# A graph kernel on one Trainium2 core: row sums and norm applications at fixed places of ScalarE's order, one eviction moved to ScalarE, one VectorE operation in four

## The chip, the cores and the metric

The kernel runs on one core of one Trainium2 chip. The core has five engines that work side by side: TensorE (PE in the profile; its weight loads are PEld), VectorE (DVE), ScalarE (ACT), GpSimd (POOL) and SyncE (SP), which here only issues DMA transfers. SBUF is the working memory, PSUM the memory that TensorE writes. The metric is the device time of one execution in microseconds (us), as the median of the runs.

## The reference

There are 64 graphs of 256 nodes with 256 features, x and adj being 64 x 256 x 256 in float32. Two layers run, each with a residual and a layer norm:

```python
# layer 0
deg = adj.sum(axis=-1); deg = jnp.where(deg != 0, deg, 1.0)
d = deg ** -0.5
a_plus = d[:, :, None] * adj * d[:, None, :] + max(alpha, MIN_VALUE) * eye
x = layernorm(x + einsum('bnf,pf->bnp', einsum('bnm,bmf->bnf', a_plus, x), W) + b)
# layer 1
h = relu(bn1(x @ conv1))                     # 1-tap convolution over features
x_conv = relu(bn2(conv17(h over nodes)) + x) # 17 taps, padding 8
s = x @ w_se.T + b_se                        # 3 columns
A = exp(-(|s_n|^2 + |s_m|^2 - 2 s_n . s_m))
msg = relu(x @ w_msg.T + b_msg)
x_in = concatenate([x_conv, A @ msg])
r, z = sigmoid(gi_r + gh_r), sigmoid(gi_z + gh_z)  # gi = x_in @ w_ih.T + b_ih, gh = x @ w_hh.T + b_hh
x = layernorm(x + (1 - z) * tanh(gi_n + r * gh_n) + z * x)
```

## The kernel before, in words

A tile has 128 partitions, so a graph's 256 nodes and its 256 features are two chunks each. The graphs go in four batches of Q = 16, because the 17-tap convolution is done through frequencies for 16 graphs at once.

`layer0(g)` is a generator, and each `yield` ends a piece. Its first piece sums adj's rows (`degrees()`, L357: two ScalarE operations of 256 columns, each followed by a read of its accumulator), corrects deg on VectorE (L368), raises it to -1/2 on GpSimd (dis, L370), takes alpha times deg (L372), transposes adj (TensorE L379, evicted by ScalarE L380), adds the diagonal (VectorE L382), scales x by dis on ScalarE (L392, twice) and adds a bias to the loaded x on GpSimd (L393). Then come p_hT (L400, evicted by L405), p_out (L410, evicted on VectorE by L415), and the layer norm. `layernorm` takes statistics on VectorE (L326 to L328), a power on GpSimd (ln_rs, L329), then ln_mr on VectorE (L332) and the application on ScalarE (L334, twice). Last, ScalarE's queue issues the store of x1 (L421).

`x1_transposed(g)` transposes the normed graph (L430) into one PSUM tile and evicts it by two operations into xn: xn's first part on VectorE (L434), or on ScalarE (L432) if the graph is in ALONE, and its last part on ScalarE (L435). `layer1(g)` multiplies by the conv weights (p_conv, L450, evicted per chunk by ScalarE as h, L453, and scols, L454), squares scols for the distances on VectorE (L458 to L461), makes messages (p_msg L471, ReLU L474), transforms to frequencies (p_dft L486, evicted by L491), transposes scols (p_rows L499, evicted as dist_l L501 and dist_r L503), takes distances (p_dist L510), their exponential (L511) and product with adj (L512), and p_nmp (L519, evicted by L523, stored by L524).

After a batch, `products` multiplies frequencies by the convolution's weights u, which are loaded from DRAM (p_k, L545; VectorE and ScalarE evict by L587 to L590, butterflies L595 and L596), `real_transform` (from L651 on, its last line L677 one VectorE operation of 8 x 256 = 2048 columns) and `complex_begin` and `complex_end` transform back, and the convolution's output goes to DRAM (xc_d). `gru(g)` then computes the gates of a graph by eight products p_g (L871) of three matmuls of 384 columns each, some on sums of blocks that GpSimd makes (L842). Its evictions are first (ScalarE L882), L888, L889, L898, L900 on VectorE, and quarter(0,0) (ScalarE L891). Tanh is on ScalarE (L913, L929), the rest on VectorE (L921 to L938). The graph's last norm is left in NORMS, and `ended()` applies it (L332, L334) and issues the store of out (L849) within the next graph's gru.

`graphs` drives a batch: for each graph it walks layer1's seven pieces, and after some of them runs a piece of layer0 of the graph two ahead (PLACES) or of other work, such as gates. After the piece APPLIED (the products for p_rows) it runs ENDS, which is layer 0's pending norm with its store. Graphs 16 to 27 (ALONE) are begun alone beside the first batch's products; graphs 32 to 37 and 48 to 53 are begun ahead beside later products, with their frequencies in a second tile V2 that L1104 copies. `paced` puts pieces of the inverse transforms behind marked operations. Within an engine a scheduler decides the order when the program is built, from the order in the program and a model of durations; the engines' queues are then fixed. `tc.issue_after(ins)` binds what is issued under it to come after ins in the order of ins's own engine. PSUM evictions share two pools of four banks; `bank` takes them in turn.

Time runs in stages: set-up with graphs 0 to 15 (to 280 us), the first products beside graphs 16 to 27 (to 460), graphs 28 to 31 with first gates (to 600), second products (to 720), gates beside graphs 32 to 37 (to 930), gates beside 38 to 47 (to 1120), the same for the third batch (to 1630), the last products (to 1720) and the last gates.

Of the kernel before, what the change touches and what calls it, by code (L numbers as in the profile page):

```python
# [10 lines left out]
AF = mybir.ActivationFunctionType  # L11
ALU = mybir.AluOpType
AX = mybir.AxisListType

P = 128
# [11 lines left out]
def kernel(  # L27
# [27 lines left out]
    nc = tc.nc  # L55
    B, N, D = x.shape
    TAPS = conv2T.shape[1]
    PAD = TAPS // 2
    NSE = w_seT.shape[1]
# [8 lines left out]
    Q = P // GT  # L68
# [22 lines left out]
    def mark(op, gates=0):  # L91
        marks.append((op.ins, gates))
# [248 lines left out]
    xn_d = [dram.tile([P, 2 * DCH, N], F32, name=f"xn_d{g}") for g in range(B)]  # L341
    XN = {}
    ALONE = set()
    ADJT, X1, X_SCALED, DIAGONAL = {}, {}, {}, {}


    def layer0(g):

        a_t, x_t = ain.pop(g), xin.pop(g)

        adjT = work.tile([P, NCH, 3, P], F32, name="adjT", bufs=3)
        ADJT[g] = adjT

        deg = small.tile([P, NCH], F32, name="deg")
        def degrees():
            for c in range(NCH):
                nc.scalar.activation(  # L357
                    unused if g >= Q else adjT[:, c, 0:2, :].rearrange("p n q -> p (n q)"), a_t[:, c, :], AF.Copy,
                    accum_out=deg[:, c : c + 1],
                )  # L360

        if g == 1:

            with tc.issue_after(X_SCALED[0]):
                degrees()
        else:
            degrees()
        nc.vector.scalar_tensor_tensor(deg, deg, 0.0, deg, op0=ALU.is_equal, op1=ALU.add)  # L368
        dis = small.tile([P, NCH], F32, name="dis")
        nc.gpsimd.tensor_tensor(dis, deg, neg_half[:, :NCH], op=ALU.pow)  # L370
        adeg = small.tile([P, NCH], F32, name="adeg")
        nc.vector.tensor_scalar(adeg, deg, alpha_t, None, op0=ALU.mult)  # L372

        p = bank("p_adjT").rearrange("p (c n) -> p c n", c=NCH)
        for mc in range(NCH):
            for c in range(NCH):
                nc.tensor.transpose(p[:, mc, c * P : (c + 1) * P], a_t[:, c, mc * P : (mc + 1) * P], ident)  # L379
        copied = nc.scalar.copy(adjT[:, :, 0:3:2, :], p.rearrange("p c (n q) -> p c n q", q=P))  # L380
        for mc in range(NCH):
            DIAGONAL[g] = nc.vector.scalar_tensor_tensor(  # L382
                adjT[:, mc, 1, :], ident, adeg[:, mc : mc + 1], adjT[:, mc, 2 * mc, :],
                op0=ALU.mult, op1=ALU.add,
            ).ins


        x1 = work.tile([P, NCH, D], F32, name="x1")
        X1[g] = x1
        with tc.issue_after(copied.ins) if g < 2 else ExitStack():  # L390
            for c in range(NCH):
                X_SCALED[g] = nc.scalar.activation(x1[:, c, :], x_t[:, c, :], AF.Copy, scale=dis[:, c : c + 1]).ins  # L392
        nc.gpsimd.tensor_tensor(x_t, x_t, b0_t.unsqueeze(1).to_broadcast([P, NCH, D]), op=ALU.add)  # L393

        yield
        hT = work.tile([P, DCH, N], F32, name="hT", bufs=1)
        p = bank("p_hT").rearrange("p (k n) -> p k n", k=DCH)
        for k in range(DCH):
            for mc in range(NCH):
                nc.tensor.matmul(  # L400
                    p[:, k, :], x1[:, mc, k * P : (k + 1) * P],
                    adjT[:, mc, 1 - mc : 3 - mc, :].rearrange("p n q -> p (n q)"),
                    start=mc == 0, stop=mc == NCH - 1,
                )
        nc.scalar.copy(hT, p)  # L405
        yield
        p = bank("p_out0").rearrange("p (c o) -> p c o", c=NCH)
        for c in range(NCH):
            for k in range(DCH):
                nc.tensor.matmul(  # L410
                    p[:, c, :], hT[:, k, c * P : (c + 1) * P], w0[:, k, :], start=k == 0, stop=k == DCH - 1
                )
        for c in range(NCH):
            mark(
                nc.vector.scalar_tensor_tensor(  # L415
                    x1[:, c, :], p[:, c, :], dis[:, c : c + 1], x_t[:, c, :], op0=ALU.mult, op1=ALU.add
                )
            )
        yield
        yield from layernorm(x1)  # L420
        nc.scalar.dma_start(x1_d[g // Q][g % Q].rearrange("(c p) d -> p c d", p=P), x1)  # L421
        yield

    def x1_transposed(g, alone=False):
        x1 = X1.pop(g)
        xn = XN[g] = work.tile([P, 2 * DCH, N], F32, name="xn")
        p = bank("p_x1T").rearrange("p (k n) -> p k n", k=DCH)
        for k in range(DCH):
            for c in range(NCH):
                nc.tensor.transpose(p[:, k, c * P : (c + 1) * P], x1[:, c, k * P : (k + 1) * P], ident)  # L430
        if alone:
            nc.scalar.activation(xn[:, 0], p[:, 0], AF.Identity, bias=unit, scale=others_only)  # L432
        else:
            nc.vector.tensor_scalar(xn[:, 0], p[:, 0], others_only, unit, op0=ALU.mult, op1=ALU.add)  # L434
        nc.scalar.copy(xn[:, 2 * DCH - 1], p[:, 1])  # L435

    def layer1(g, place):
# [3 lines left out]
        xn, adjT = XN.pop(g), ADJT.pop(g)  # L441
# [5 lines left out]
        for c in range(NCH):  # L447
            p = bank("p_conv1")[:, : D + NSE]
            for k in range(DCH):
                nc.tensor.matmul(  # L450
                    p, x1T[:, k, c * P : (c + 1) * P], wc1[:, k, :], start=k == 0, stop=k == DCH - 1
                )
            nc.scalar.activation(h[:, c, :], p[:, :D], AF.Relu)  # L453
            nc.scalar.copy(cols[:, c, :, :NSE], p[:, D:].unsqueeze(1).to_broadcast([P, 4, NSE]))  # L454

        s3 = cols[:, :, 0, :NSE]
        sq3 = small.tile([P, NCH, NSE], F32, name="sq3")
# [11 lines left out]
        for c in range(NCH):  # L469
            for k in range(DCH):  # L470
                nc.tensor.matmul(  # L471
                    p[:, c, :], x1T[:, k, c * P : (c + 1) * P], wmsg[:, k, :], start=k == 0, stop=k == DCH - 1
                )
        mark(nc.scalar.activation(msg, p, AF.Relu))  # L474
        yield


# [34 lines left out]
        mark(nc.vector.tensor_mul(aT, aT, adjT[:, :, 0:3:2, :]))  # L512
        yield
        if g in ALONE:
            x1_transposed(g + 1, True)
        p = bank("p_nmp").rearrange("p (k n) -> p k n", k=DCH)
        for k in range(DCH):
            for mc in range(NCH):
# [132 lines left out]
    def real_transform():  # L651


        sub2(M[:, 0:3:2, :], M[:, 1:4:2, :])
        yield

        sub2(M[:, 4:6, :].rearrange("p a o -> p (a o)"), M[:, 6:8, :].rearrange("p a o -> p (a o)"))
        add2(M[:, 6, :], M[:, 7, :])
        r = math.sqrt(0.5)
        for i, by in enumerate((-1.0, 1.0, -r, r)):  # L660
            stt(M[:, 4 + i, :], M[:, 4 + i, :], by, M[:, i, :], op0=ALU.mult, op1=ALU.add)
        stt(M[:, 0:4, :], M[:, 0:4, :], 2.0, M[:, 4:8, :], op0=ALU.mult, op1=ALU.subtract)
        yield

        run(four(8, 12))
        yield
        nc.vector.tensor_sub(M[:, 8, :], M[:, 0, :], M[:, 8, :])
        nc.vector.tensor_add(M[:, 12, :], M[:, 4, :], M[:, 12, :])
        for i, x, y in ((1, 9, 13), (2, 10, 14), (3, 15, 11)):
            angle = math.pi * ORDER[i] / 8  # L670
            t = freq.tile([P, 2, D], F32, name="turn", bufs=2)
            by = real_part(t[:, 0, :], M[:, x, :], M[:, y, :], angle)
            imaginary_part(t[:, 1, :], M[:, x, :], M[:, y, :], angle)
            stt(M[:, 8 + i, :], t[:, 0, :], -by, M[:, i, :], op0=ALU.mult, op1=ALU.add)
            stt(M[:, 12 + i, :], t[:, 1, :], by, M[:, 4 + i, :], op0=ALU.mult, op1=ALU.add)
            yield
        stt(M[:, 0:8, :], M[:, 0:8, :], 2.0, M[:, 8:16, :], op0=ALU.mult, op1=ALU.subtract)  # L677
        yield

    CR, CI = 16, 32  # L680
# [170 lines left out]
    def ended():  # L851
        while NORMS:
            run(NORMS.pop(0))

    def gru(g):
# [21 lines left out]
        def quarter(c, h):  # L877
            return G[:, c, h].rearrange("p t d -> p (t d)")
# [9 lines left out]
        mark(nc.vector.tensor_add(quarter(0, 1), first, p6), 1)  # L888
        nc.vector.tensor_add(quarter(1, 1), quarter(0, 1), p7)  # L889
        product(A12, B21, p1)  # L890
        nc.scalar.copy(quarter(0, 0), p1)  # L891
        yield
        if following:
            transposed(g + 1)
        ended()
        load_x1(g)
        p5 = product(S[1], T1)
        mark(nc.vector.tensor_add(quarter(1, 1), quarter(1, 1), p5), 1)  # L898
# [69 lines left out]
    def run(stage):  # L968
        for _ in stage:
            pass  # L970
# [21 lines left out]
    def graphs(first, part, others):  # L992


        for i in part:
            load(first + i + 3)
            given = {"layer0": layer0(first + i + 2) if first + i + 2 < B else iter(()), "other": others[i]}
            for piece, _ in enumerate(layer1(first + i, i)):
                if piece == APPLIED:
                    run(ENDS.pop())  # L1000
                    ENDS.append(given["layer0"])
                elif piece == STATS:
                    next(given["layer0"], "end")
                yield
                for name in PLACES[piece]:
                    if next(given[name], "end") != "end":
                        yield
            yield from given["other"]
# [203 lines left out]
```

## Time and profile before

| | |
|---|---|
| three runs | 2105.25, 2107.64, 2108.99 us, median 2107.64 |
| profiled execution | 2108.64 us |
| its span | 2106.8 us, so 1.8 around it |
| granted TensorE clock | 0.989 |
| matmuls | 8157 |
| L357 on the unused tile | 96 of 0.415 us, and 96 reads of 0.189 |
| L334 on x, on x_g | 128 of 0.601, 128 of 0.596 us |
| L434 (VectorE), L432 (ScalarE) | 52 of 0.533, 12 of 0.564 us |
| L677, L596 with 512 columns | 4 of 2.286, 68 of 0.755 us |
| L370 (dis), L392 | 64 of 0.719, 128 of 0.509 us |

Times are those of one profiled execution, in us from the start of its span. A busy share is the time in which an engine ran instructions. In the view of waits a line names the engine that stood still and its instruction, then who released it, and the total, the number and the longest of such waits. A timeline has a line for each instruction or run of alike ones: start, duration, engine, line of the kernel, what it writes and reads, how many, and in brackets the idle time ahead of it with its releaser. TensorE's ends are modelled, so that a matmul that waits inside a run shows as a longer run.

### The profile page before, as it was taken

The page shows a single profiled execution, that of the slowest core. Times are in us where ns is not written, and L with a number is a line of the kernel's source. Part 1 is how long each engine was busy: PE and PEld are TensorE (multiplying, and loading weights), DVE is VectorE, ACT ScalarE, POOL GpSimd, SP SyncE. Part 2 cuts the span into 40 slices and gives each one's busy share as a digit, 9 for nine tenths or more (in the row PEclk, how much of TensorE's full clock was granted, in tenths as well). Part 3 has the DMA queues.
Part 4 walks back from the last instruction along what each step waited for, and adds up shares of the span by engine and source line. Part 5 has one row for each costly group of instructions (what it writes and reads, how often), then busy time and mean ns, then how long its engine had stood idle before and what let it go on. Part 6 is the DMA issues. An engine that isn't in the chain of part 4 may idle for free. (4 is left out here: it accounts for less than half of the span.)

```text
span 2106.8 us, 26312 instructions
## 1 busy us (share of the span) xinstructions
PE 2004.8 (95%) x8157; PEld 1444.7 (69%) x8157; DVE 1437.3 (68%) x3281; ACT 923.4 (44%) x2180; POOL 668.0 (32%) x672
## 2 busy tenths in 40 slices
PE   6999999999999999999999999999999999999997
PEld 5888778877677766767677666667767765555554
DVE  5545467776567788863446888875444899976776
ACT  4666643566431234455453123546544123333333
POOL 3444410122332243322322234323222124434442
PEclk9999999999999999999999999999999999999999
DMA  4765557545346644343326655434322845443331
GB/s 125 226 217 183 190 173 228 176 140 155 92 149 201 203 126 120 115 118 108 101 86 189 195 155 140 120 110 120 109 83 90 254 142 147 115 117 97 93 94 54
DMA packets 305289, 298.05 MB, mean 141 GB/s; under 512 B 84192, under 2 KB 283956, under 8 KB 305150
## 3 DMA queue, kind: packets, MB, share of 16 engines
q1 hardware_dynamic: 245198, 200.37, 32.7%
q10 hardware_dynamic: 44480, 67.39, 9.0%
q0 software_dynamic: 15472, 28.61, 6.2%
q8 instruction: 66, 1.08, 0.2%
q14 instruction: 73, 0.60, 0.1%
HBM read 193.19 MB, written 103.06 MB: 141 GB/s over the span
## 5 line engine op out<-in xcount | busy, mean ns | idle before, releaser
L871 PE MATMUL p_g<-wall,sums 128*128 128x384 f32 x1536 | 541.4, 493 | 8.0 <-DVE G L898 8.0
L871 PEld LDWEIGHTS p_g<-wall,sums 128*128 128x128 f32 x1536 | 286.3, 192 | 199.4 <-issue 17.6
L871 PE MATMUL p_g<-wall,inputs 128*128 128x384 f32 x1152 | 406.3, 489 | 14.5 <-DVE G L889 13.8
L871 PEld LDWEIGHTS p_g<-wall,inputs 128*128 128x128 f32 x1152 | 216.9, 190 | 167.0 <-DVE G L889 22.9
L842 POOL TENSOR_TENSOR sums<-inputs 128x384 f32<-128x384 f32 x128 | 139.9, 1094 | 344.2 <-PE p_g L871 315.5
L329 POOL TENSOR_TENSOR ln_rs<-ln_rs,neg_half 128x2 f32<-128x2 f32 x129 | 94.9, 736 | 384.8 <-DVE ln_rs L328 297.7
L913 ACT ACTIVATE G<-G 128x512 f32<-128x512 f32 x128 | 80.6, 630 | 260.6 <-DVE G L900 144.6
L545 PE MATMUL p_k<-u,VM 128*128 128x256 f32 x736 | 175.9, 381 | 4.0 <-DMA u<-ud 3.8
L545 PEld LDWEIGHTS p_k<-u,VM 128*128 128x128 f32 x736 | 139.4, 191 | 31.4 <-DMA u<-ud 3.7
L450 PE MATMUL p_conv<-wc,xn 128*128 128x259 f32 x512 | 128.0, 390 | 14.0 <-DVE xn L434 13.1
L370 POOL TENSOR_TENSOR dis<-deg,neg_half 128x2 f32<-128x2 f32 x64 | 46.0, 719 | 293.6 <-DVE deg L368 293.4
L393 POOL TENSOR_TENSOR x_t<-x_t,b_t 128x512 f32<-128x512 f32 x64 | 94.3, 1473 | 135.5 <-issue 112.1
L400 PE MATMUL p_hT<-adjT,x 128*128 128x256 f32 x512 | 127.3, 391 | 8.4 <-DVE adjT L382 4.7
L512 DVE TENSOR_TENSOR aT<-aT,adjT 128x512 f32<-128x512 f32 x64 | 45.6, 712 | 124.4 <-ACT aT L511 124.3
L486 PE MATMUL p_dft<-fwd,h 128*128 128x240 f32 x512 | 117.4, 372 | 10.6 <-ACT scols L454 10.6
L410 PE MATMUL p_out<-w,hT 128*128 128x256 f32 x512 | 123.7, 384 | 2.7 <-ACT hT L405 2.1
L450 PEld LDWEIGHTS p_conv<-wc,xn 128*128 128x128 f32 x512 | 96.6, 193 | 40.3 <-DVE xn L434 17.6
L519 PE MATMUL p_nmp<-aT,msg 128*128 128x256 f32 x512 | 121.4, 380 | 0.2 <-DVE aT L512 0.2
L471 PE MATMUL p_msg<-wmsg,xn 128*128 128x256 f32 x512 | 121.5, 380 | 0.0
L334 ACT ACTIVATE x_g<-x_g,ln_mr,ln_rs 128x256 f32<-128x256 f32 x128 | 70.8, 596 | 111.0 <-DVE ln_mr L332 106.7
L410 PEld LDWEIGHTS p_out<-w,hT 128*128 128x128 f32 x512 | 95.9, 191 | 30.5 <-ACT hT L405 11.9
L842 POOL TENSOR_TENSOR sums<-inputs,sums 128x384 f32<-128x384 f32 x64 | 70.2, 1097 | 142.0 <-PE p_g L871 141.6
(164 smaller groups left out, 3578.2 us busy)
## 6 DMA issues: line engine op xcount, KB each, us to landing
u<-ud SPq DMA_DIRECT2D x284, 256.0 KB
xn_d<-xn ACTq DMA_DIRECT2D x64, 512.0 KB
inputs<-xn_d SPq DMA_DIRECT2D x64, 512.0 KB
ud<-u_set POOLq DMA_DIRECT2D x39, 480.0 KB, 6.2
adj_t<-in_adj_dram SPq DMA_DIRECT2D x64, 256.0 KB
x_t<-in_x_dram SPq DMA_DIRECT2D x64, 256.0 KB
x_d<-x ACTq DMA_DIRECT2D x64, 256.0 KB
xc_d<-VM SPq DMA_DIRECT2D x64, 256.0 KB
```

The lines of the kernel that those rows point to most:

```text
L329: nc.gpsimd.tensor_tensor(rs[:, : len(chunks)], rs[:, : len(chunks)], neg_half[:, : len(chunks)], op=ALU.pow)
L393: nc.gpsimd.tensor_tensor(x_t, x_t, b0_t.unsqueeze(1).to_broadcast([P, NCH, D]), op=ALU.add)
L400: nc.tensor.matmul(p[:, k, :], x1[:, mc, k * P : (k + 1) * P], adjT[:, mc, 1 - mc : 3 - mc, :].rearrange("p n q -> p (n q)"), start=mc == ...
L410: nc.tensor.matmul(p[:, c, :], hT[:, k, c * P : (c + 1) * P], w0[:, k, :], start=k == 0, stop=k == DCH - 1)
L450: nc.tensor.matmul(p, x1T[:, k, c * P : (c + 1) * P], wc1[:, k, :], start=k == 0, stop=k == DCH - 1)
L471: nc.tensor.matmul(p[:, c, :], x1T[:, k, c * P : (c + 1) * P], wmsg[:, k, :], start=k == 0, stop=k == DCH - 1)
L486: nc.tensor.matmul(p[:, t0 * FL : t1 * FL], h[:, c, k * P : (k + 1) * P], fwd[:, first : first + t1 - t0, :].rearrange("p t f -> p (t f)") ...
L519: nc.tensor.matmul(p[:, k, :], msg[:, mc, k * P : (k + 1) * P], aT[:, mc].rearrange("p n q -> p (n q)"), start=mc == 0, stop=mc == NCH - 1,)
L545: nc.tensor.matmul(p[:, j * D : (j + 1) * D], v[:, k, :], u[:, k, :], start=k == 0, stop=k == DCH - 1)
L842: nc.gpsimd.tensor_tensor(S[i], x, y, op=op)
L871: nc.tensor.matmul(p[:, : 3 * HD] if k == 0 else p[:, HD:], a[:, k], wall[:, b, k].rearrange("p t d -> p (t d)"), start=first and k == 0, ...
L913: nc.scalar.activation(rz, rz, AF.Tanh, scale=0.5)
```

## The change

Five things change. First, the row sums of layer 0 of graph g, where g is at least 16 and g - 2 is not in ALONE (graphs 16, 17 and 30 to 63), are bound on ScalarE behind the last scols eviction of layer1(g - 2). Second, layer 0's norm application with its store is bound behind the message ReLU of the graph under work. Third, the gates' norm application with the store of out is bound behind the copy of quarter(0,0). Fourth, xn's first part is always evicted by ScalarE. Fifth, L677's operation is issued as four of 512 columns. Lines after the first hunk lie one to three further down than before.

In the changed kernel ScalarE issues 52 activations more (L432's form, 64 in place of 12), VectorE 52 fewer (L434) and 12 more (L677, 16 in place of 4); TensorE, GpSimd and SP issue as many as before.

```diff
@@ -341,6 +341,7 @@
     ALONE = set()
+    EVICTED, RELU = {}, {}
@@ -359,9 +360,9 @@
-        if g == 1:
-
-            with tc.issue_after(X_SCALED[0]):
+        if g == 1 or g >= Q and g - 2 not in ALONE:
+
+            with tc.issue_after(X_SCALED[0] if g == 1 else EVICTED[g - 2]):
                 degrees()
         else:
             degrees()
@@ -421,17 +422,14 @@
-    def x1_transposed(g, alone=False):
+    def x1_transposed(g):
...
-        if alone:
-            nc.scalar.activation(xn[:, 0], p[:, 0], AF.Identity, bias=unit, scale=others_only)
-        else:
-            nc.vector.tensor_scalar(xn[:, 0], p[:, 0], others_only, unit, op0=ALU.mult, op1=ALU.add)
+        nc.scalar.activation(xn[:, 0], p[:, 0], AF.Identity, bias=unit, scale=others_only)
         nc.scalar.copy(xn[:, 2 * DCH - 1], p[:, 1])
@@ -451,7 +449,7 @@
-            nc.scalar.copy(cols[:, c, :, :NSE], p[:, D:].unsqueeze(1).to_broadcast([P, 4, NSE]))
+            EVICTED[g] = nc.scalar.copy(cols[:, c, :, :NSE], p[:, D:].unsqueeze(1).to_broadcast([P, 4, NSE])).ins
@@ -471,7 +469,9 @@
-        mark(nc.scalar.activation(msg, p, AF.Relu))
+        relu = nc.scalar.activation(msg, p, AF.Relu)
+        RELU[g] = relu.ins
+        mark(relu)
@@ -512,7 +512,7 @@
         if g in ALONE:
-            x1_transposed(g + 1, True)
+            x1_transposed(g + 1)
@@ -674,7 +674,8 @@
-        stt(M[:, 0:8, :], M[:, 0:8, :], 2.0, M[:, 8:16, :], op0=ALU.mult, op1=ALU.subtract)
+        for i in range(0, 8, 2):
+            stt(M[:, i : i + 2, :], M[:, i : i + 2, :], 2.0, M[:, 8 + i : 10 + i, :], op0=ALU.mult, op1=ALU.subtract)
@@ -888,11 +889,12 @@
-        nc.scalar.copy(quarter(0, 0), p1)
+        own = nc.scalar.copy(quarter(0, 0), p1).ins
...
-        ended()
+        with tc.issue_after(own):
+            ended()
@@ -997,7 +999,8 @@
                 if piece == APPLIED:
-                    run(ENDS.pop())
+                    with tc.issue_after(RELU[first + i]):
+                        run(ENDS.pop())
```

## The prediction

> **What bounds the kernel now.** I read the page's busy shares first, then the view of waits, then the timelines of ScalarE, TensorE, VectorE and GpSimd around the waits that end on TensorE.
>
> ```profile
> PE 2004.8 (95%) x8157; PEld 1444.7 (69%) x8157; DVE 1437.3 (68%) x3281; ACT 923.4 (44%) x2180; POOL 668.0 (32%) x672
> ```
>
> TensorE (PE) is the bound, so only its stalls can be won. Its busy time hides some of them, so I took the starts of successive matmuls from its timeline and compared each step with the median of its shape (0.323 us for p_g, 0.216 for 256 columns, 0.218 p_conv, 0.203 p_dft, 0.109 a transpose). All that lies over 0.06 us above the median sums to 137.5 us; without it the matmuls would take 1988.5. I gave each late step to the instruction that released it, and call that its excess below.
>
> The view of waits names the releasers (total us, times, longest):
>
> ```profile
> ACT x_g L334 <- DVE ln_mr L332: 106.7, 49, 5.1
> ...
> ACT unused L357 <- DMA adj_t<-in_adj_dram: 32.3, 19, 3.8
> ...
> PEld p_conv L450 <- DVE xn L434: 17.6, 13, 2.6
> ...
> PE p_conv L450 <- DVE xn L434: 13.1, 12, 2.4
> PEld p_dist L510 <- ACT dist_r L503: 12.9, 15, 3.5
> ...
> PE p_dft L486 <- ACT scols L454: 10.6, 7, 2.2
> ```
>
> TensorE waits for evictions, and ScalarE (ACT), 44% busy, waits for norms (L334) and loads (L357) that nobody needs yet. ScalarE's timeline (start, duration, and in brackets the idle time before and who ended it) shows both:
>
> ```profile
> 1009.25 1.09 ACT L334 ACTIVATE x<-x,ln_mr,ln_rs 128x256 f32<-128x256 f32 x2 [4.64 <-DVE ln_mr L332]
> 1010.25 0.36 ACT L453 ACTIVATE h<-p_conv 128x256 f32<-128x256 f32 x1
> ...
> 1035.59 0.42 ACT L357 ACTIVATE unused<-adj_t 128x256 f32<-128x256 f32 x1 [1.66 <-DMA adj_t<-in_adj_dram]
> ...
> 1036.74 0.37 ACT L503 COPY dist_r<-p_rows 64x256 f32<-64x256 f32 x1
> ```
>
> and TensorE's shows what they cost:
>
> ```profile
> 1010.72 3.35 PE L486 MATMUL p_dft<-fwd,h 128*128 128x240 f32 x8 [2.16 <-ACT scols L454]
> ...
> 1037.16 0.70 PE L510 MATMUL p_dist<-dist_r,dist_l 32*128 32x256 f32 x4 [0.99 <-ACT dist_r L503]
> ```
>
> The application at 1009.25 held h's eviction, and so p_dft, for 2.16 us; the row sum at 1035.59 held dist_r, and so p_dist, for 0.99.
>
> **What the Trainium skill says.** "TensorE: Matmul & The Clock Gate", section on the array's architecture: the queues of ScalarE and VectorE are strictly in order. The trace agrees: the 1010.25 eviction ran only after the norm. The same page, on clock oscillation: TensorE falls to half its clock after some 3.4 us idle. The trace agrees in kind, at a slightly shorter gap: the six p_g matmuls that follow a 2.98 us stall at 1190.56 take 2.94 us, and six undisturbed ones 2.10. "GPSIMD Engine Reference", specifications: GpSimd shares its SBUF interfaces with VectorE. The trace agrees: a 12-element operation of VectorE (L458) took 1.24 us instead of 0.17 at 854.15, under an L393 of GpSimd that was stretched from a mean of 1.47 to 4.39.
>
> **Part by part: what goes.**
> - *x1 transposed.* The excess on p_conv behind VectorE's L434 is 15.8 us: 7.7 in the first 280 us, 8.1 later. ScalarE's own form L432 costs 0.564 against 0.533. The second copy L435 already waits for the first (35.7 us in 43 waits), so the pair stays serial: 0.46 + 0.37 on ScalarE after the change, 0.53 + 0.37 now. The queue of VectorE drops out, and what is late next is a p_conv behind ScalarE's queue. I take 15.0 of the 15.8. ScalarE's 52 more operations at a step of 0.46 are 24 us of busy time in 1183 idle ones.
> - *Norms at fixed places.* Behind an L334 that waits for ln_mr, p_dft has an excess of 11.8 (seven places), and p_hT, which takes the PSUM bank that the message ReLU frees, 4.3. Both go if the norms stand after that ReLU and after L891. The store of x1 (L421) moves with the one and the store of out (L849) with the other, both on ScalarE's queue. x1_d is read by the same graph's gates, after its batch's products, and out by nobody, so they cost nothing under that cover; without it a gate load would come later by the few us of the move. ln_mr (L332) stays in VectorE's order. SP's loads and GpSimd's ln_rs only trade near places in the built order; I cost that at nothing, too, as each load has some window to spare. By L891 the ln_mr of the graph before is long there. What is late next is L491, now with one L334 between its two copies: 0.49 us, inside the timeline below.
> - *Row sums.* p_dist and p_out behind an L357 that waits for adj_t have an excess of 11.4 us; without the early L357 I take 7.0 of p_dist's 10 (the rest stands behind L491 and the copies of L1104) and all 1.4 of p_out.
> - *The operation in four.* One 2048-column operation takes 2.286 us, four of 512 columns 4 x 0.755 = 3.02 (row of L596): 0.73 more, four times, so 2.9 us more on VectorE, against 27.7 us that L434's 52 leave. For it a waiting eviction gets in earlier; the place is here:
>
> ```profile
> 1184.82 2.28 DVE L677 SCALAR_TENSOR_TENSOR VM<-VM 128x2048 f32<-128x2048 f32 x1
> ...
> 1189.83 0.67 DVE L889 TENSOR_TENSOR G<-G,p_g 128x512 f32<-128x512 f32 x1
> ```
>
>   L889 released the 2.98 us stall. Two such stalls (680 and 1190 us) can shrink; I take 3.5. The other 20 or so us behind L889 and L898, most of them after 1720, stand in VectorE's order of gates, which the change leaves.
> - *Slow clock.* After the long stalls at 569, 904, 1192 and 1416 p_g runs at about 0.64 a step for up to five steps. With the stalls shorter I take 3.0.
>
> Gone: 15.0 + 11.8 + 4.3 + 7.0 + 1.4 + 3.5 + 3.0 = 46.0 us.
>
> **What comes.** Now the row sums of a graph run about a window ahead of their use:
>
> ```profile
> 1016.50 0.70 POOL L370 TENSOR_TENSOR dis<-deg,neg_half 128x2 f32<-128x2 f32 x1 [7.30 <-DVE deg L368]
> ```
>
> and the L392 that uses this dis starts at 1024.90. After the change 36 graphs (16, 17, 30 to 63) have them after scols of the graph two before, in the window in which L392 and p_hT need them, so a chain over three engines falls between p_conv and p_hT. By ScalarE's issue steps, from the start of p_conv: h's second eviction at 1.94, scols 2.22, L357 2.27, adjT's L380 2.68, second L357 3.16 to 3.67, deg (VectorE) 3.70 to 3.86, dis (GpSimd, 0.70) 3.94 to 4.64, L392 at 4.67 and 5.08, message ReLU 5.49 to 6.08, so p_hT at 6.13. TensorE is there after p_conv 1.75, adjT 0.44, p_msg 1.73, p_dft 1.62 and p_rows 0.22: at 5.75. Stall: 0.38. The queue behind the waiting L392 is the ReLU, L491, dist_l and dist_r; the last comes at 7.9 for a p_dist due at 7.86, so about 0.05 more. Where an L842 of GpSimd (1.00) runs just before deg, which it does for about every second graph, it adds some 0.45. Mean 0.6 us. Graphs 32 and 48 have their chain spread over product work; 34 windows x 0.6 = 20.4 us.
>
> Bounds: no stall where the ReLU stands ahead of L392 (the built order has that in a dozen windows), so 0.2 us or 7 in all; above, a deg behind one more 0.68 operation of VectorE and a dis behind one 1.27 us L393 give 0.6 + 0.68 + 1.27, over 2.5 us in a window and up to 1.9 as a mean, 65 in all. I take 20.4.
>
> **Sum.** 46.0 - 20.4 = 25.6 us less. The profiled execution took 2108.64 (span 2106.8, 1.8 around it), so 2083.0; it lies 1.0 above the median of the runs, so 2082.0. A measurement of this kernel can tell some 0.2%, 4.2 us, from no change.
>
> **Rivals.**
> - *The chain becomes the wait (slower).* Price: the same 34 windows. It decides from 46.0 / 34 = 1.35 us each. For it: from 720 to 930 us VectorE is 80% busy (167.6 of 210), and L393 has been stretched to 4.39 us just there; each engine serves its queue in order, and deg and dis stand in two of them. Against it: most windows lie where VectorE is less busy (89.5 of 190 us from 930 to 1120). At 1.9 us: 64.6 - 46.0 = 18.6 more, 2126.2 in the median.
> - *The stalls change their releaser (same).* For it: p_hT already waits 4.7 us for adjT's diagonal (L382, VectorE), p_k for u's loads, p_g for L889. If half of the 46.0 comes back behind those, 23.0 - 20.4 = 2.6 less: 2105.0.
> - *The chain is hidden.* At 0.15 us a window 5.1 come in: 40.9 less, 2066.7. For it: the dozen windows with the ReLU first. Against it: the 0.38 above is there with every engine free.
>
> **Chances.** Forecast 0.60 (its own range 2070 to 2098), hidden chain 0.13, same 0.12, chain as the wait 0.15. Faster by over 0.2%: 0.60 + 0.13 = 0.73; within: 0.12; slower: 0.15. The range 2062 to 2116 takes in the forecast, most of the hidden chain, the same case, and the least of the slower one.
>
> **What would show it.** In the changed kernel's waits: L434 gone as a releaser of p_conv; "L334 <- DVE ln_mr" far below 168 us (106.7 for x_g and 61.3 for x); "L357 <- DMA adj_t" near none; new waits of L392 for dis L370, some 1 us in some 30 windows, and with them of p_hT for the message ReLU, together near 20 us. If those pass 46 us, or if L382 and L889 hold what L434 and L454 held, I am wrong.

## The result, and the profile after

The changed kernel takes 2078.44 us (median of 4 runs, 2074.1 to 2084.28), the kernel before 2108.31 beside it: a ratio of 0.987, 95% interval 0.9844 to 0.9896. A later set of runs gave 0.9876 (0.9854 to 0.9897). The forecast was 2082.0. The profiled execution took 2079.83, its span 2078.0: 28.8 less than before.

The busy shares of the changed kernel:

```profile
PE 1996.5 (96%) x8157; PEld 1444.4 (70%) x8157; DVE 1395.1 (67%) x3241; ACT 937.4 (45%) x2232; POOL 663.7 (32%) x672
```

TensorE's late steps, taken as the prediction takes them, sum to 108.9 us, 137.5 before. That is 28.6 less, so they hold nearly the whole of the span's change. The waits of the changed kernel (total, times, longest) show which:

```profile
ACT x_g L334 <- DVE ln_mr L332: 53.0, 34, 3.3
...
ACT x L393 <- POOL dis L371: 47.3, 39, 3.4
...
ACT x L334 <- DVE ln_mr L332: 16.1, 6, 3.6
...
PEld p_dist L510 <- ACT dist_r L503: 13.0, 34, 1.2
...
PE p_hT L401 <- ACT x L393: 7.7, 9, 1.8
PEld p_conv L448 <- ACT xn L432: 7.5, 8, 1.3
ACT unused L358 <- DMA adj_t<-in_adj_dram: 7.5, 3, 3.6
...
PE p_conv L448 <- ACT xn L432: 5.7, 7, 1.1
...
PE p_hT L401 <- ACT msg L472: 4.7, 18, 0.8
...
PE p_dft L486 <- ACT scols L452: 1.9, 1, 1.9
```

L334's waits for ln_mr fell from 168 to 69 us and those for adj_t from 32.3 to 7.5. L434 is gone as a releaser. L393's waits for dis rose from 4 (6.7 us) to 39 (47.3), those of p_hT for the ReLU from 7 (3.1 us) to 18 (4.7), and p_hT now waits 9 times for L393 itself (7.7). The new chain can be read off ScalarE's, GpSimd's and TensorE's timelines of one window of the changed kernel (start, duration, and in brackets the idle time before and its releaser). The window's p_conv starts at 993.53:

```profile
995.76 0.16 ACT L452 COPY scols<-p_conv 128x12 f32<-128x12 f32 x1
995.81 0.43 ACT L358 ACTIVATE unused<-adj_t 128x256 f32<-128x256 f32 x1
...
996.22 0.58 ACT L381 COPY adjT<-p_adjT 128x512 f32<-128x512 f32 x1
996.69 0.43 ACT L358 ACTIVATE unused<-adj_t 128x256 f32<-128x256 f32 x1
...
998.22 0.91 ACT L393 ACTIVATE x<-x_t,dis 128x256 f32<-128x256 f32 x2 [1.00 <-POOL dis L371]
999.03 0.57 ACT L472 ACTIVATE msg<-p_msg 128x512 f32<-128x512 f32 x1
```

```profile
997.49 0.69 POOL L371 TENSOR_TENSOR dis<-deg,neg_half 128x2 f32<-128x2 f32 x1 [0.79 <-DVE deg L369]
```

```profile
993.53 1.91 PE L448 MATMUL p_conv<-wc,xn 128*128 128x259 f32 x8
...
999.66 1.56 PE L401 MATMUL p_hT<-adjT,x 128*128 128x256 f32 x6 [0.20 <-ACT msg L472]
```

Counted from 993.53, L358 starts at 2.28, L381 at 2.69, the second L358 at 3.16, dis at 3.96, L393 at 4.69, the ReLU at 5.50, and p_hT at 6.13. The prediction had 2.27, 2.68, 3.16, 3.94, 4.67, 5.49 and 6.13. The late step is 0.37 (0.38), of which the trace books 0.20 as idle.

### The profile page after: what moved, and what is told of

Same layout as the page of the kernel before. It is cut to its first block, busy times and chain, and to the rows that moved or that the text cites. A ratio compares the mean times of both kernels' runs of the same rounds, so it can differ in the third digit from the quotient of the medians.

```text
span 2078.0 us, 26334 instructions
## 1 busy us (share of the span) xinstructions
PE 1996.5 (96%) x8157; PEld 1444.4 (70%) x8157; DVE 1395.1 (67%) x3241; ACT 937.4 (45%) x2232; POOL 663.7 (32%) x672
## 4 chain that ended last, share of the span: by engine, by line
PE 48%; DVE 12%; issue 4%; DMA 4%; POOL 3%; ACT 3%; SPq 0%; ACTq 0%; POOLq 0%; DVEq 0%
PE p_g L872 30%; PE p_k L545 7%; PE p_hT L401 3%; PE p_out L411 2%; PE p_nmp L519 2%; DMA u<-ud 2%; POOL sums L843 1%; DVE ln_st L326 1%; PE p_dist L510 1%; PE p_conv L448 1%; DVE VM L733 1%; ACT x L393 1%; POOL dis L371 1%; POOL ln_rs L329 1%; DVE G L927 1%
## 5 line engine op out<-in xcount | busy, mean ns | idle before, releaser
L843 POOL TENSOR_TENSOR sums<-inputs 128x384 f32<-128x384 f32 x128 | 142.7, 1115 | 317.7 <-PE p_g L872 265.6
L512 DVE TENSOR_TENSOR aT<-aT,adjT 128x512 f32<-128x512 f32 x64 | 47.3, 740 | 229.1 <-ACT aT L511 229.1
L394 POOL TENSOR_TENSOR x_t<-x_t,b_t 128x512 f32<-128x512 f32 x64 | 89.5, 1399 | 158.5 <-issue 92.1
L401 PEld LDWEIGHTS p_hT<-adjT,x 128*128 128x128 f32 x512 | 95.2, 197 | 40.2 <-ACT x L393 10.7
L843 POOL TENSOR_TENSOR sums<-inputs,sums 128x384 f32<-128x384 f32 x64 | 68.9, 1077 | 133.9 <-PE p_g L872 133.8
```

Source lines behind the costliest of these rows:

```text
L401: nc.tensor.matmul(p[:, k, :], x1[:, mc, k * P : (k + 1) * P], adjT[:, mc, 1 - mc : 3 - mc, :].rearrange("p n q -> p (n q)"), start=mc == ...
L843: nc.gpsimd.tensor_tensor(S[i], x, y, op=op)
```

## The experiments

All were timed against the kernel before on the same chip. "Excess" is what the prediction calls so, by the tile of the late matmul. A ratio's interval is some 0.0020 to each side, 4 us, so a single part of 5 us is settled by the trace and not by the time. A trace is of one execution, the first of its run; where it lies more than 5 us from the run's median, this is said. In all fourteen traces the span less the late steps is 1968.2 to 1969.6 us, so the late steps hold what differs between two of them. The order of every engine is built anew for each kernel, so an experiment takes away a part together with what the new order brings elsewhere.

**One part alone, on the kernel before.**

*x1T_only*: ScalarE makes both evictions.

```diff
-        if alone:
-            nc.scalar.activation(xn[:, 0], p[:, 0], AF.Identity, bias=unit, scale=others_only)
-        else:
-            nc.vector.tensor_scalar(xn[:, 0], p[:, 0], others_only, unit, op0=ALU.mult, op1=ALU.add)
+        nc.scalar.activation(xn[:, 0], p[:, 0], AF.Identity, bias=unit, scale=others_only)
```

> The kernel before with both evictions of x1's transposes on ScalarE, no other part. The forecast's term: p_conv's excess falls by 15.0, from 20.6 to about 6, 2090. Rival, from the changed kernel: L432 waits behind L523 on ScalarE in the windows without gates (0.87 us each), so p_conv keeps 8.7, 11 to 12 less, 2093; or, in ScalarE's queue with free norms and row sums, it waits behind them and brings less than 5, 2100.

2088.03 us, ratio 0.9923 (0.9903 to 0.9944), 16 us less. p_conv's excess fell from 20.6 to 8.4, so the rival's account of p_conv is the right one: L432 behind L523 keeps 0.87 us in some windows without gates. The time fell by the forecast's 15 nevertheless, because other stalls moved too (p_dft 14.4 to 6.0, p_g 39.1 to 34.6, against p_out 7.3 to 11.6).

*norms_only*: both norm applications bound.

```diff
+        with tc.issue_after(own):
+            ended()
...
+                    with tc.issue_after(RELU[first + i]):
+                        run(ENDS.pop())
```

> The kernel before with the two norm applications' edges alone. The forecast's terms: p_dft's 11.8 us and p_hT's 4.3 behind L334 go, 16.1 less than the kernel before, about 2088. Rival: the 17 and 23 us that each edge was worth in the changed kernel are worth of both together with the row sums' edge (a late norm starts the chain late), and alone the two bring less than 10: 2095 or more.

2091.72, ratio 0.9939 (0.992 to 0.9958), 13 us less. p_dft's excess fell from 14.4 to 2.6 as forecast; p_hT's didn't fall (16.3 to 18.3). The first theory holds for p_dft, and the rival does not. p_dist's fell as well, from 16.1 to 9.0, although the row sums are free here.

*rows_only*: the row sums' edge alone.

```diff
-        if g == 1:
+        if g == 1 or g >= Q and g - 2 not in ALONE:
 
-            with tc.issue_after(X_SCALED[0]):
+            with tc.issue_after(X_SCALED[0] if g == 1 else EVICTED[g - 2]):
```

> The kernel before with the row sums' edge alone, no other part. Theory from the run with free row sums: the edge trades a chain of some 17 us ahead of p_hT for the waits for adj_t on ScalarE (about 8 us of p_dist and p_out) and for the waits of deg in VectorE's queue, which delayed the gates' evictions (4.5 us of p_g), and some of the slow clock: 2101 to 2106, against 2106 for the kernel before. Rival (the forecast's own terms, 20.4 in against 8.4 out): some 10 us slower than the kernel before, 2116.

2115.01, ratio 1.0044 (1.0025 to 1.0063): 9 us slower, as the rival says. p_hT's excess rose from 16.3 to 40.4, more than the forecast's 20.4. But the traced execution took 2107.13, the least of thirteen, and its late steps sum to 135.8, no more than the 137.5 before: p_dist, p_dft and p_g have 8.2, 7.0 and 6.9 us less. So the time shows that the edge alone costs, and the trace doesn't show that it costs by the forecast's terms.

**One part undone in the changed kernel** (ratio 0.987).

*x1T_vector*: the diff of x1T_only, the other way.

> The changed kernel, with xn's first part evicted by VectorE again outside ALONE. Theory: p_conv's excess rises from 8.7 to about 20, and the 4.5 us of stalls of p_g behind VectorE between 720 and 800 and between 1240 and 1320, which the change removed beyond the forecast, come back, since L434's 52 operations stood in VectorE's queue there: about 2094. Rival: those p_g stalls went for another reason (the order of the norms), so 2085 to 2090 and p_g's excess stays at 23.

2088.33, ratio 0.9921 (0.9901 to 0.9941), some 11 us worth. p_conv's excess went back to 22.0, but p_g's stalls of 720 to 815 and 1200 to 1325 did not come back (1.3 us there, 5.4 before). The rival holds in that L434 had not been their cause; the cause that it names, the order of the norms, is not it either, since norms_only keeps them (5.5).

*no_split*: L677 whole.

```diff
-        for i in range(0, 8, 2):
-            stt(M[:, i : i + 2, :], M[:, i : i + 2, :], 2.0, M[:, 8 + i : 10 + i, :], op0=ALU.mult, op1=ALU.subtract)
+        stt(M[:, 0:8, :], M[:, 0:8, :], 2.0, M[:, 8:16, :], op0=ALU.mult, op1=ALU.subtract)
```

> The changed kernel, with L677 one operation of 2048 columns again. Theory: the two stalls of p_g behind it (at 680 and 1190 us before, 1.7 and 3.1) come back: 4.5 us with the slow clock after them, 2082 to 2083. Rival: they had gone because L434 left VectorE, and the time stays at 2078, with p_g's excess at 23.

2081.0, ratio 0.9892 (0.9872 to 0.9912). The time alone cannot tell that from 0.987, but the trace can. VectorE and TensorE of this run:

```profile
1170.50 2.29 DVE L677 SCALAR_TENSOR_TENSOR VM<-VM 128x2048 f32<-128x2048 f32 x1
```

```profile
1176.24 3.71 PE L871 MATMUL p_g<-wall,inputs 128*128 128x384 f32 x6 [2.99 <-DVE G L889]
```

The stall is back, and the six matmuls behind it take 3.71 us in place of 2.10. p_g's excess in the two places (600 to 720 and 1110 to 1200) is 7.6 with one operation and 0.4 with four. Every kernel with one operation has 5.5 to 9.7 there, every kernel with four 0.4 to 0.9. For the kernel as a whole little comes of it: all late steps of this trace sum to 109.7, against 108.9 with four, because others are smaller here, and the times differ by less than their intervals. In the trace of the changed kernel the four lie spread among other work (one starts at 1164.90, the other three at 1169.77), at 0.68 us each:

```profile
1169.77 1.88 DVE L678 SCALAR_TENSOR_TENSOR VM<-VM 128x512 f32<-128x512 f32 x3
```

Three in a row take 1.88 us, so one starts 0.60 after another. Four in a row would take some 2.5 us against 2.29 for the whole, an estimate from this line: the 0.73 more that the prediction allowed came from adding durations that overlap.

*rows_free*: the diff of rows_only, the other way.

> The changed kernel, with the row sums of graphs 16, 17 and 30 to 63 free again (no edge behind scols). Theory: the chain from the row sums over deg and dis to L393 costs p_hT about 17 us in the changed kernel (excess 33.3 against 16.3 before), and free row sums cost p_dist and p_out about 8 us through their wait for adj_t. So p_hT's excess falls to about 14, p_dist's rises by some 7, and the time falls from 2078 to about 2069. Rival: the edge is a gain in all, since an early row sum that waits for adj_t blocks all of ScalarE's queue; then this kernel is slower than the changed one, at about 2085 to 2090.

2084.27, ratio 0.9904 (0.9881 to 0.9928). Not the 2069 of my theory, and nearer the rival's number than mine; the intervals of this and the changed kernel overlap, and the late steps of the two traces sum to 108.5 and 108.9 (this run's traced execution is its shortest, 2078.84). What the edge is worth in the changed kernel is thus not settled. p_hT's excess did fall, from 33.3 to 20.9, but p_rows rose from 5.5 to 12.1 (two stalls of 4.0 near 932 and 1429) and p_g from 22.9 to 28.0; p_dist rose by 1.7, not by the 7 expected. The stalls of p_rows stand in VectorE's queue too:

```profile
929.89 0.94 DVE L332 SCALAR_TENSOR_TENSOR ln_mr<-ln_mv,ln_rs 128x2 f32<-128x2 f32 x1 [1.12 <-POOL ln_rs L329]
...
931.14 0.78 DVE L459 TENSOR_SCALAR scols<-nsq 128x4 f32<-128x4 f32 x1
```

```profile
932.07 0.41 PE L499 MATMUL p_rows<-ident,scols 128*128 128x128 f32 x2 [3.83 <-DVE scols L459]
```

The norm's ln_mr, whose place in VectorE's order the change leaves free, waits for GpSimd ahead of the distances that p_rows needs. The same wait stands in the changed kernel, where the two stalls are of 2.13 us. Here ln_rs before it (L328) takes 1.87 us in place of 0.15, beside GpSimd's L394 (927.11 to 928.37).

The rise of p_g is what x1T_vector left open. In all four kernels with free row sums (before, x1T_only, norms_only, this one) it has 5.4 to 5.5 us in 720 to 815 and 1200 to 1325, and in all nine with bound ones 0.6 to 2.4. The timelines of ScalarE, VectorE and TensorE of the kernel before show how:

```profile
789.96 0.42 ACT L357 ACTIVATE unused<-adj_t 128x256 f32<-128x256 f32 x1 [3.83 <-DMA adj_t<-in_adj_dram]
```

```profile
791.04 0.16 DVE L368 SCALAR_TENSOR_TENSOR deg<-deg 128x2 f32<-128x2 f32 x1 [2.86 <-ACT unused L357]
```

```profile
795.70 2.20 PE L871 MATMUL p_g<-wall,inputs 128*128 128x384 f32 x6 [0.85 <-DVE G L889]
```

A load that is late by 3.83 us holds a row sum, the row sum holds deg and with it VectorE's queue for 2.86 us, and less than five microseconds on p_g waits for a gate's eviction in that queue (L889); VectorE has no idle time in between. All four kernels have such a wait of deg, of 2.6 to 2.9 us, near 790 and near 1290, and the changed kernel has none. The total of VectorE's waits for the row sums doesn't tell them apart: it is 99.5 us before, 20.0 in the changed kernel and 22.3 in this one. The p_g steps right behind these waits hold some 3.0 of the 5.4 us of the kernel before. Others, near 740 and 1240 (1.1 us each in this run), have no waiting deg ahead of them; in this run VectorE's L933 takes 1.64 us before both in place of 0.69, beside GpSimd's L394 (736.00 to 737.60 at the first).

*norm0_free* and *normg_free*: one of the two norm edges undone (layer 0's, and the gates').

```diff
-                    with tc.issue_after(RELU[first + i]):
-                        run(ENDS.pop())
+                    run(ENDS.pop())
```

> The changed kernel, with layer 0's norm application free again (no edge behind the message ReLU), the gates' application still bound. Theory: most of the 12 us that p_dft lost behind L334, and p_hT's 4, came from this application, so p_dft's excess rises from 2.2 to about 10, and the time to about 2088. Rival: with the x1 evictions away from VectorE and the row sums late, ln_mr comes early enough, and the time stays within 3 us of the changed kernel.

```diff
-        with tc.issue_after(own):
-            ended()
+        ended()
```

> The changed kernel, with the gates' norm application free again (no edge behind quarter(0,0)), layer 0's still bound. Theory: this one waited the longer time for ln_mr (106.7 us of ScalarE before, against 61.3), but mostly where nothing stood behind it: p_dft's excess rises by 4 and the time to about 2083. Rival: it is the main one of the two, and the time rises by 10 to about 2088.

2095.82, ratio 0.9956 (0.9943 to 0.997), and 2101.75, ratio 0.9985 (0.9972 to 0.9997): 18 and 24 us worth, each more than the two bring alone. The second exceeds even its rival. p_dft rose about as forecast (2.2 to 8.2, and to 10.0), and p_hT far more than forecast (33.3 to 48.4, and to 44.5). The traced execution of norm0_free is the longest of its run, 2104.77, so its 48.4 is on the high side; that of normg_free is at the median. ScalarE and TensorE of normg_free, at the window shown above:

```profile
994.21 1.09 ACT L334 ACTIVATE x_g<-x_g,ln_mr,ln_rs 128x256 f32<-128x256 f32 x2 [3.96 <-DVE ln_mr L332]
...
996.41 0.45 ACT L358 ACTIVATE unused<-adj_t 128x256 f32<-128x256 f32 x1
```

```profile
996.26 1.89 PE L486 MATMUL p_dft<-fwd,h 128*128 128x240 f32 x8 [1.33 <-ACT scols L452]
...
1000.27 1.99 PE L401 MATMUL p_hT<-adjT,x 128*128 128x256 f32 x8 [1.91 <-ACT msg L472]
```

The norm that waits for ln_mr now holds the row sums too, and so starts the chain late: p_hT's late step is 2.08 us in every second window from here to 1085, and 0.37 in the changed kernel. The bound row sums need the bound norms.

**Other places for the same instructions.**

*rows_early*: the row sums a window earlier, after the exponentials.

```diff
-            nc.scalar.activation(aT[:, c].rearrange("p n q -> p (n q)"), p, AF.Exp, bias=nsq[:, c : c + 1], scale=2.0)
+            EXPS[g] = nc.scalar.activation(aT[:, c].rearrange("p n q -> p (n q)"), p, AF.Exp, bias=nsq[:, c : c + 1], scale=2.0).ins
...
-            with tc.issue_after(X_SCALED[0] if g == 1 else EVICTED[g - 2]):
+            with tc.issue_after(X_SCALED[0] if g == 1 else EXPS[g - 3]):
```

> The changed kernel, with the row sums of those 36 graphs bound behind the last exponential (L511) of the graph three before, in place of scols of the graph two before: about a window earlier than in the changed kernel, and later than where they waited for adj_t before. Theory (chain): deg, dis and L393 are done before p_conv of the window in which p_hT needs them, L358 finds adj_t loaded, p_hT's excess falls from 33 to about 14, p_dist's stays near 9: about 2060. Rival (the stalls change their releaser): p_hT then waits for adjT's diagonal (L383) or for the ReLU, which come at nearly the same time, and little is won: 2074 or more.

2076.44, ratio 0.9869 (0.9847 to 0.989). The theory's own step was right: p_hT's excess fell from 33.3 to 13.5. But the time hardly moved, since p_dist rose by 7.5 and p_out by 4.9. ScalarE of this run shows by what:

```profile
569.02 0.51 ACT L821 ACTIVATE inputs<-inputs,bn_bias 128x256 f32<-128x256 f32 x1 [6.79 <-POOL inputs L818]
569.56 0.58 ACT L406 COPY hT<-p_hT 128x512 f32<-128x512 f32 x1
...
934.95 0.60 ACT L334 ACTIVATE x<-x,ln_mr,ln_rs 128x256 f32<-128x256 f32 x1 [3.63 <-DVE ln_mr L332]
```

The ReLU on the gates' inputs stood ahead of hT's eviction, and layer 0's norm ahead of L491 and dist_r. The late step of p_out was 4.79 us, and that of p_dist 3.56, twice. The stalls changed their releaser, as the rival says, though not to the releaser it names.

*rows_norm_exp* moves layer 0's norm behind the exponential too (inside ALONE it stays behind the message ReLU), and *all_exp* the gate inputs' ReLU as well:

```diff
+                elif piece == APPLIED + 1 and first + i not in ALONE:
+                    with tc.issue_after(EXPS[first + i]):
+                        run(ENDS.pop())
+                    ENDS.append(given["layer0"])
```

```diff
+            with tc.issue_after(EXPS[max(EXPS)]):
+                for k in range(DCH):
+                    nc.scalar.activation(xcT[:, k], xcT[:, k], AF.Relu, bias=bn2_bias[:, k : k + 1])
```

> As the run all_exp, without the edge on the gate inputs' ReLU (L821). Theory: the waits of hT's eviction behind L821, 4.8 us at 570 and some 1.3 elsewhere, come back: about 2065. Rival: with the norm out of the way, L821 falls elsewhere, and it stays at 2060.

> The changed kernel, with three places moved: the row sums behind the last exponential (L511) of the graph three before, layer 0's norm application behind the exponential of the graph under work (outside ALONE), and the ReLU on the gates' inputs (L821) behind the last exponential issued. Theory: after the exponential ScalarE is idle for some 3 us in every window, so these wait at no cost; what held p_hT (chain and ReLU), p_dist (L334 between L491's copies, 3.6 us twice near 935 and 1430) and p_out (4.8 us at 570 behind L821) in the earlier runs goes: some 20 us below the changed kernel, 2056 to 2062. Rival: the stalls change their releaser again (VectorE's L383 and L459, the gates' evictions), and it stays at 2070 or above.

*rows_norm_exp*: 2079.02, ratio 0.9872 (0.985 to 0.9893), no better than the changed kernel: neither the 2065 of the theory nor the 2060 of its rival came. Its traced execution took 2071.43, the least of six, so the trace explains the median in part only. In it L821's waits for GpSimd are 72.1 us, one of 6.35 standing ahead of dist_r at 929.89; p_rows has 10.1 us of excess. *all_exp*: 2059.81, ratio 0.9782 (0.9761 to 0.9803), as expected and 19 us faster than the changed kernel. L821's waits are 38.2. Its ScalarE and TensorE, in a window like the one above:

```profile
995.31 0.84 ACT L511 ACTIVATE aT<-p_dist,nsq 128x256 f32<-128x256 f32 x2
996.04 1.08 ACT L334 ACTIVATE x<-x,ln_mr,ln_rs 128x256 f32<-128x256 f32 x2
...
998.50 0.42 ACT L358 ACTIVATE unused<-adj_t 128x256 f32<-128x256 f32 x1
...
999.38 0.58 ACT L893 COPY G<-p_g 128x512 f32<-128x512 f32 x1 [0.37 <-PE p_g L873]
```

```profile
992.54 0.38 PE L499 MATMUL p_rows<-ident,scols 128*128 128x128 f32 x2
992.75 1.89 PE L401 MATMUL p_hT<-adjT,x 128*128 128x256 f32 x8
```

Norm, ReLU and row sums fit between the exponentials and the next eviction that TensorE needs, and even leave 0.37 us of idle time. p_hT follows p_rows without a gap. All late steps sum to 85.1 us. Some 16 of them are p_g after 1640, where every kernel here has 15 to 20.

*after_again* is the changed kernel beside three of these.

> The changed kernel itself, on the same chip as the three others, so that they can be compared with it: 0.987 of the kernel before, 2074 to 2081.

2078.62, ratio 0.9876 (0.9854 to 0.9897), as expected.

## Why the prediction was right, point by point

Forecast and trace by the excess of the waiting tile, in us:

| tile | forecast | before to after | difference |
|---|---|---|---|
| p_conv | -15.0 | 20.6 to 8.7 | -11.9 |
| p_dft | -11.8 | 14.4 to 2.2 | -12.2 |
| p_dist | -7.0 | 16.1 to 9.1 | -7.0 |
| p_hT | -4.3 + 20.4 | 16.3 to 33.3 | +17.0 |
| p_out | -1.4 | 7.3 to 9.9 | +2.6 |
| p_g | -3.5 - 3.0 | 39.1 to 22.9 | -16.2 |
| others | 0 | 23.7 to 22.8 | -0.9 |
| sum | -25.6 | 137.5 to 108.9 | -28.6 |

- **x1 transposed** was right in kind and too large by 3: L432 stands behind L523 in windows without gates (0.87 us, five times) and in two others (1.25 each). I had let the queue of ScalarE cost 0.8 in all. One of the five, in the changed kernel:

```profile
238.93 0.58 ACT L523 COPY xn<-p_nmp 128x512 f32<-128x512 f32 x1 [2.41 <-PE p_nmp L519]
239.41 0.57 ACT L432 ACTIVATE xn<-p_x1T,ident,others_only 128x256 f32<-128x256 f32 x1
```

```profile
240.03 1.14 PE L448 MATMUL p_conv<-wc,xn 128*128 128x259 f32 x4 [0.70 <-ACT xn L432]
```

- **Norms** were right for p_dft, though other parts alone bring it down as well (x1T_only to 6.0, rows_only to 7.4). Their worth was underrated: undone one at a time they cost 18 and 24 us, because the new chain starts behind them. My sum added parts that are not independent.
- **Row sums**: p_dist's 7.0 came out to the digit, but not by the row sums' edge alone: with the norms' edges and free row sums it is as low (9.0 in norms_only), and undoing the row sums' edge brings back only 1.7. Either part takes away its longest late step, 3.31 us at 568. p_out was wrong in sign. Of its rise of 2.6, 2.2 are ten steps near 935 and 1437, 0.13 to 0.32 us late each without idle time, in a slow stretch (shown at the end); 0.5 is an eviction of hT that stands right behind L334 (a late step of 0.83 at 510, 0.30 before). Left out was VectorE: the prediction named what is queued behind a waiting L357 on ScalarE, but not what is queued behind the waiting deg. p_g fell by 4.8 us in the two places of rows_free (5.4 to 0.6), some 3.0 of it right behind a waiting deg.
- **The chain** was right to 0.02 us in the plain window, and its sum came near in part by luck. For the 36 graphs p_hT's excess went from 7.5 to 24.4. The 21 windows in which L393 stands ahead of the ReLU, as in the forecast's timeline, have 9.5 of these, mostly a late step of 0.37 or 0.38. The 15 with the ReLU ahead, for which the prediction saw no stall, have 14.9 (some 2.5 of it slow steps), with late steps of up to 1.97: L393 waits up to 2.83 us for dis there, and in nine of the fifteen p_hT waits for L393 itself. The 0.45 for an L843 ahead of deg is not there in the plain window either (L843 ends at 996.70, before deg is due).
- **The split** gave 5.1 where I took 3.5 (p_g in its two places 5.5 to 0.4), slow clock included; what of it stays in the whole is open (no_split). The rest of p_g's 16.2 is mostly the first 600 us (3.9 to 0.3), which holds the slow steps after 569 us. One reading of the prediction was wrong here, without weight in the sum: the operation of VectorE that took 1.24 us at 854.15 has 6 elements to a partition (128x6), not 12.
- **The rivals.** The chain did not become the wait as a whole, but the row sums' edge without the rest of the change is slower by 9 us, with 24.1 more on p_hT. The stalls did change their releaser, in rows_early and rows_norm_exp and not in the changed kernel.

The two errors that count, p_g (9.7 more than forecast) and p_out with p_conv (7.1 less), partly cancel, so that the total came nearer than its terms.

## What to carry to other kernels

An in-order engine that is 44% busy can still set the pace: for each instruction that waits on it, ask who stands behind, on this engine and on those that its result goes to. Fixing one instruction's place can move the wait to the next one that is early, so fix all that can be early, and put them where the engine is idle and nobody waits for what comes next. Parts that share a queue are not additive: undo each in the whole as well as trying each alone.

## What had not been expected

Executions of one kernel spread more than 0.2%: the kernel before ran from 2095.34 to 2115.77 us over 49 executions in one set of runs. And slow TensorE steps come after less idle time than the 3.4 us that the Trainium skill names ("TensorE: Matmul & The Clock Gate", the section on clock oscillation): in no_split four p_g steps after 2.99 us are 0.32 to 0.48 us late each, and in the changed kernel 1.96 and 0.79 us of idle time, with two short matmuls between them, were enough. In another execution of the same kernel, after_again, nearly the same stall was followed by full speed. First the changed kernel, then after_again:

```profile
926.03 0.51 PE L499 MATMUL p_rows<-ident,scols 128*128 128x128 f32 x2 [1.96 <-DVE deg L369]
927.33 3.78 PE L401 MATMUL p_hT<-adjT,x 128*128 128x256 f32 x8 [0.79 <-ACT x L393]
```

```profile
928.43 0.41 PE L499 MATMUL p_rows<-ident,scols 128*128 128x128 f32 x2 [1.96 <-DVE deg L369]
929.72 1.99 PE L401 MATMUL p_hT<-adjT,x 128*128 128x256 f32 x8 [0.89 <-ACT x L393]
```

So the length of a stall alone doesn't tell whether slow steps follow. Steps without idle time that take 1.7 to 2.2 times their tile's median cost, after the first 100 us, an estimated 11.9 us in the kernel before, 6.3 in the changed kernel and 0.2 in all_exp, a part of what fewer stalls are worth. On p_g alone it is 4.4 before and 1.5 after, where the forecast took 3.0 off.
